# A four-layer graph network on one core: loads reordered, TensorE transposes chosen by site, and the last ten sample pairs scheduled side by side

## The chip, the cores and the metric

The kernel runs on one core of a Trainium2 chip. A core has TensorE (PE, matmuls and transposes, results in PSUM), VectorE (DVE), ScalarE (ACT), GpSimd (POOL) and the queue of SyncE (SP), which here issues every DMA transfer. Each engine runs its own instructions strictly in the order in which they were written out, and waits on semaphores for the others. The metric is the device time of one execution in microseconds (us), the median of several runs.

## The reference

The input x is 64 samples of 256 nodes with 128 features, in fp32, and adj is one 256x256 weighted adjacency matrix. Four layers follow one another, each `x = layernorm(x + f(x, adj))`:

```python
# layer 0: gated graph network, 5 steps
m = adj @ h                                    # used as both m_in and m_out
z = sigmoid([m, m] @ w3.T + b3 + h @ u3.T + bu3)
r = sigmoid([m, m] @ w4.T + b4 + h @ u3.T + bu3)
hv = tanh([m, m] @ w5.T + b5 + (r * h) @ u5.T + bu5)
h = (1 - z) * h + z * hv
# layer 1: semantic graph convolution, A = softmax of edge values over rows
out = (A * I) @ (x @ W[0]) + (A * (1 - I)) @ (x @ W[1]) + bias
# layer 2: attention over the edges of adj, then a graph isomorphism layer
h = x @ Wp + bp
attn = softmax(leaky(s_src + s_dst) where adj > 0)
g = relu(layernorm((attn * adj) @ h))
z = relu(layernorm(((1 + eps) * g + adj @ g) @ W1 + b1))
out = relu(z @ W2 + b2 + g)
# layer 3: polynomials of adj up to the third order
y = sum_k (adj^k @ x) @ V_k                    # k = 0..3
```

## The kernel before

**Tiles.** Two samples make a pair, so there are 32 pairs. A pair's state is a 128x512 fp32 tile: two samples, two halves of the nodes, 128 features. Products with adj need the nodes on the partitions, products with weights need the features there, so a tile is often turned (its four 128x128 blocks transposed).

**A turn** (`turn`, L440 to L479) is made in one of two ways. Through DMA: DVE transposes 32x32 blocks (L467), a transfer writes the tile to a DRAM buffer (L469), four transfers read its blocks back in the turned order (L475). On PE: four transposes against the identity into a PSUM bank (L461), then a copy to SBUF by ACT (L202) or DVE (L203). The sites of turns are named: `h` (the new state after each of layer 0's first four steps), `y` (after the fifth), `x1` (layer 1; on PE it uses `transposes`, L437, and its consumer L629 reads PSUM with no copy), `x2` and `w` (layer 2; `w` is the attention, 1024 columns, two turns), `z` (layer 2's hidden state), `x3` (layer 3). `by_dma` (L449) decides. Before the change all sites of pairs 0 to 29 go through DMA, all sites of pairs 30 and 31 are on PE.

**Stages on PE**, by line:

- L486, `spread`: a product with a 256x256 matrix (adj transposed is `aT`, layer 1's is `offT`, layer 2's is `ginT`).
- L580, L581, L588, L595, L596: layer 0's gate matmuls, 512 columns each; five steps.
- L617, `products`: weights of layer 1 and 2, 128 columns.
- L645: layer 2's first product. L686: attention times features.
- L724, L725, L732: layer 3 (`vx`, `vq`, and `a2T`, the square of adj).

Around them: L584, L590, L598 are the tanh on ACT, L586, L600, L601, L603 the gates' arithmetic on DVE, L500 to L521 and L538 to L567 the layer norms (statistics on DVE or ACT, the power on POOL, the scaling on DVE, ACT or POOL), L654 to L673 the attention's scores, largest value, leaky step and exponential, L691 to L707 the vector work of layer 2, L738 the store of the result.

**Order.** Every operation is added to one list, with its pair, one or more ways (engine and planned duration), the values it reads and writes. `Schedule.order` (L109) then plays the list with those planned durations: again and again it takes, of all operations whose inputs are planned to be ready, the one that can start first, and writes the instructions out in that order. Where two can start together, the smaller `due(pair) - rest` goes first. `rest` is the planned length of what hangs on the operation within its pair. `due` is 20 per pair, but 10 for the last 8 pairs (`DUE`, `LAST_DUE`, `LAST`, L41). An operation that may run on several engines takes the one where it would end first. `MARGIN` stretches planned durations on all engines but PE, and `LAG` is added to what one engine needs to see another's result.

**Buffers.** `CLASSES` (L34) gives the number of tiles: X holds the pairs' states, T their loaded transposes, A the working tiles, B the attention tiles of 1024 columns, E the DRAM buffers of turns, PS the eight PSUM banks. An operation that needs a tile waits in the plan until one is free.

**Start.** `load` (L226) puts the inputs on the SP queue: aT, x of the first pair, W0 (the weights of layer 0), xT of the first pair, the bias columns, pairs 1 and 2, adj, W1 (the other weights), rows. That is the order in which they are added. All have pair -1, whose due is -10000, and the order among them follows `rest`, which puts W0 and the columns ahead. `WARM` dummy matmuls (L255) keep PE active until inputs are there.

Of the kernel before, what the change touches and what calls it, by code (L numbers as in the profile page):

```python
# [14 lines left out]
D = 128  # L15
STEPS = 5

BY_DMA = ("h", "y", "x1", "x2", "w", "z", "x3")
BY_PE = 2

WARM = 6

TURN, TT = 0.44, 0.61
LN_EPS = 1e-5
# [6 lines left out]
N_L0 = 8  # L31
# [1 line left out]
ROWS = ["l1_bias", "bp", "b1", "gat_g", "gat_b", "b2"]  # L33


CLASSES = {"X": (512, 12), "T": (512, 3), "A": (512, 34), "H": (520, 5), "B": (1024, 8), "S": (32, 64), "PS": (512, 8), "D": (512, 4), "E": (1024, 8)}

SEEN = {"PE": 0.23, "ACT": 0.16, "DVE": 0.16, "POOL": 0.12, "SP": 2.5}

USES = {"DVE+": ("DVE", "PORT"), "POOL": ("POOL", "PORT")}  # L40


DUE, LAST_DUE, LAST = 20.0, 10.0, 8

MARGIN, LAG = 1.06, 0.8


def mm(cols):
# [30 lines left out]
class Schedule:  # L79
# [20 lines left out]
        return op  # L100

    def due(self, pair):
        if pair < 0:
            return -1e4
        late = max(pair - (self.n_pairs - LAST), 0)
        return DUE * (pair - late) + LAST_DUE * late

    def order(self, tiles):
        for op in self.ops:  # L109
            op.waits = len(op.before)  # L110
            for b in op.before:
                b.then.append(op)
            for v in dict.fromkeys([*op.reads, *op.writes]):
                v.left += 1
        for op in reversed(self.ops):
            us = min(w[1] for w in op.ways) + op.seen
            op.rest = us + max((x.rest for x in op.then if x.pair == op.pair), default=0.0)
        free = {cls: [(0.0, t) for t in ts] for cls, ts in tiles.items()}
        engines = dict.fromkeys([*SEEN, "PORT"], 0.0)
        ready = [op for op in self.ops if not op.waits]  # L120
        out = []
        while ready:
            best = None
            for op in ready:
                held = 0.0
                for v in op.writes:
                    if v.cls and v.ap is None:
                        held = max(held, min((t for t, _ in free[v.cls]), default=1e9))
                if held == 1e9:
                    continue  # L130
                for engine, us, fn in op.ways:
                    us = us if engine == "PE" else us * MARGIN
                    start = max(op.ready, held, *(engines[e] for e in USES.get(engine, (engine,))))
                    key = (start + (us if len(op.ways) > 1 else 0.0), self.due(op.pair) - op.rest, op.number)
                    if best is None or key < best[0]:
                        best = key, start, op, engine, us, fn
            if best is None:
                raise RuntimeError("no operation can start: too few tiles")
            _, start, op, engine, us, fn = best
            ready.remove(op)  # L140
            for v in op.writes:
                if v.cls and v.ap is None:
                    slot = min(free[v.cls], key=lambda s: s[0])
                    free[v.cls].remove(slot)
                    v.ap = slot[1]
            end = start + us
            engines.update(dict.fromkeys(USES.get(engine, (engine,)), end))
            out.append((start, op.number, op, fn))
            for v in dict.fromkeys([*op.reads, *op.writes]):
                v.left -= 1  # L150
                v.end = max(v.end, end + op.seen)
                if not v.left and v.cls:
                    free[v.cls].append((v.end, v.ap))
            for x in op.then:
                x.waits -= 1
                same = engine != "SP" and x.ways[0][0].rstrip("+") == engine.rstrip("+")
                x.ready = max(x.ready, end + (0.0 if same else op.seen))
                if not x.waits:
                    ready.append(x)

            for v in dict.fromkeys([*op.reads, *op.writes]):
                op.__dict__.setdefault("tiles", {})[v] = v.ap
        assert len(out) == len(self.ops), "operations that wait for one another"
        self.span = max(engines.values())
        return [(op, fn) for _, _, op, fn in sorted(out, key=lambda x: x[:2])]
# [3 lines left out]
def kernel(ctx: ExitStack, tc: tile.TileContext, x, xT, adj, adjT, mats, cols, rows, out):  # L169
    nc = tc.nc  # L170
    n_pairs = x.shape[0] // 2
# [4 lines left out]
    S = Schedule(n_pairs)  # L176

    def fixed(shape, name):
        return Value(ap=const.tile([P, *shape], F32, name=name), name=name)

    def pe(us, fn, r, w):
        S.add([("PE", us, fn)], r, w)
# [4 lines left out]
    def dve(us, fn, r, w):  # L187
        S.add([("DVE", us, fn)], r, w)
# [19 lines left out]
    W0, W1 = fixed([N_L0, D], "W0"), fixed([len(MATS) - N_L0, D], "W1")  # L208
    ccol = fixed([len(COLS)], "ccol")
# [13 lines left out]
        i = ROWS.index(name)  # L223
        return rbc.ap[:, None, i * D:(i + 1) * D].to_broadcast([P, n, D])

    def load(o, i, v):  # L226
        S.add([("SP", 0.4, lambda: nc.sync.dma_start(o(), i))], [], [v])

    xs = [Value("X", name=f"x{p}") for p in range(n_pairs)]
    hTs = [Value("T", name=f"hT{p}") for p in range(n_pairs)]  # L230
# [1 line left out]
    def load_x(p):  # L232
        load(lambda: xs[p].at(4, D), x[2 * p:2 * p + 2].rearrange("b (t p) d -> p (b t) d", p=P), xs[p])
        load(lambda: hTs[p].at(2, N), xT[2 * p:2 * p + 2].rearrange("b d n -> d b n"), hTs[p])
# [3 lines left out]
    dve(0.2, lambda: nc.vector.tensor_scalar(ident.ap, diff.ap, 0.0, None, op0=ALU.is_equal), [diff], [ident])  # L238
    dve(0.1, lambda: nc.vector.memset(neg_half.ap, -0.5), [], [neg_half])
    load(lambda: aT.ap, adjT.rearrange("(t p) i -> p t i", p=P), aT)  # L240
    load(lambda: xs[0].at(4, D), x[0:2].rearrange("b (t p) d -> p (b t) d", p=P), xs[0])
    load(lambda: W0.ap, mats[:, :N_L0], W0)
    load(lambda: hTs[0].at(2, N), xT[0:2].rearrange("b d n -> d b n"), hTs[0])
    load(lambda: ccol.ap, cols, ccol)
    for p in range(1, 3):
        load_x(p)
    load(lambda: a.ap, adj.rearrange("(t p) j -> p t j", p=P), a)
    load(lambda: W1.ap, mats[:, N_L0:], W1)
    load(lambda: rbc.ap, bass.AP(tensor=rows.tensor, offset=rows.offset, ap=[[0, P], [1, n_rows]]), rbc)


# [1 line left out]
    dve(0.3, lambda: nc.vector.memset(ones.ap, 1.0), [], [ones])  # L253
    for _ in range(WARM):
        pe(0.87, lambda: nc.tensor.matmul(idle.at(N), ones.ap[:, :P], ones.ap, start=True, stop=True), [ones], [idle])  # L255
# [191 lines left out]
        return v  # L447

    def by_dma(site):  # L449
        return site in BY_DMA and S.pair < n_pairs - BY_PE  # L450

    def turn(i, name, site, n=512):


        o = Value("A", name=name) if n == 512 else i
        if not by_dma(site):
            ts = [Value("PS", name="ps") for _ in range(n // 512)]
            for k, t in enumerate(ts):
                def fn(k=k, t=t):
                    for c in range(4):  # L460
                        nc.tensor.transpose(tokens(t)[:, c, :], i.at(n // P, P)[:, 4 * k + c, :], ident.ap)  # L461
                pe(TURN, fn, [i, ident], [t])
            for k, t in enumerate(ts):
                evacuate(lambda k=k: o.at(n)[:, 512 * k:512 * k + 512], lambda t=t: t.at(512), [t], [o])
            return o
        st, d = Value("A" if n == 512 else "B", name="turn"), Value("E", name="turn")
        dve(n / 512 * 0.55 + 0.09, lambda: nc.vector.transpose(st.at(n), i.at(n)), [i], [st])  # L467
        blocks = lambda *ap: bass.AP(tensor=d.ap.tensor, offset=d.ap.offset, ap=ap)
        S.add([("SP", 0.4, lambda: nc.sync.dma_start(blocks([P, P], [P * P, n // P], [1, P]), st.at(n // P, P)))],  # L469
              [st], [d], n / 512 * 0.7 + 1.3)  # L470

        def move():
            for q in range(4):
                b = blocks([P, 32], [32 * P, n // 32], [1, 32])
                nc.sync.dma_start(o.at(n // 32, 32)[32 * q:32 * q + 32],  # L475
                                  bass.AP(tensor=b.tensor, offset=b.offset + 32 * q, ap=b.ap))
        S.add([("SP", 2.1, move)], [d], [o], n / 512 * 1.5 + 1.9)
        return o
# [271 lines left out]
    tiles = {}  # L750
    for cls, (n, count) in CLASSES.items():
        where = {"PS": psum, "D": dram, "E": dram}.get(cls, shared)
# [47 lines left out]
```

## Time and profile before

| | |
|---|---|
| time, median of 3 (lowest to highest) | 1554.17 us (1551.33 to 1554.42) |
| span of the profiled run | 1547.6 us |
| PE, DVE, ACT, POOL busy | 1525.6, 1201.5, 868.7, 372.2 us |
| mean granted PE clock | 0.997 |
| DMA traffic | 210.47 MB, 136 GB/s on average |
| HBM read, written | 113.97 MB, 94.96 MB |

An engine's busy time divided by the span is its share. PE's records overlap, since matmuls are pipelined, so its busy time is an upper bound of its work. The page's slices give the busy share of each fortieth of the span in tenths. The chain of waits is followed back from the last instruction and tells which engine's work, at each moment, had to be over for the end to come when it did. A wait names the engine that stood, the line and tile of the instruction that waited, and the one that released it. The windows give each engine's busy time in stretches of the span. Traffic is mostly the turns: each writes 256 KB to DRAM and reads it back.

### The profile page before, as it was taken

The page shows a single profiled execution, that of the slowest core. Times are in us where ns is not written, and L with a number is a line of the kernel's source. Part 1 is how long each engine was busy: PE and PEld are TensorE (multiplying, and loading weights), DVE is VectorE, ACT ScalarE, POOL GpSimd, SP SyncE. Part 2 cuts the span into 40 slices and gives each one's busy share as a digit, 9 for nine tenths or more (in the row PEclk, how much of TensorE's full clock was granted, in tenths as well). Part 3 has the DMA queues.
Part 4 walks back from the last instruction along what each step waited for, and adds up shares of the span by engine and source line. Part 5 has one row for each costly group of instructions (what it writes and reads, how often), then busy time and mean ns, then how long its engine had stood idle before and what let it go on. Part 6 is the DMA issues. An engine that isn't in the chain of part 4 may idle for free.

```text
span 1547.6 us, 22483 instructions
## 1 busy us (share of the span) xinstructions
PE 1525.6 (99%) x6356; PEld 1060.9 (69%) x6356; DVE 1201.5 (78%) x2879; ACT 868.7 (56%) x2363; POOL 372.2 (24%) x467
## 2 busy tenths in 40 slices
PE   9999999999999999999999999999999999999987
PEld 6556666666776666677766677766667767777886
DVE  5556768888888868777788777878787878899874
ACT  3444445566655565565655665565555555667752
POOL 0000110022333121221222222221322312445632
PEclk9999999999999999999999999999999999999999
DMA  7434557777678767677777677877666854557541
GB/s 216 106 72 97 107 113 150 158 146 147 145 165 164 166 134 149 139 145 144 165 145 149 148 132 150 158 144 155 150 137 138 165 114 102 125 107 144 108 92 48
DMA packets 917788, 210.47 MB, mean 136 GB/s; under 512 B 702752, under 2 KB 913184, under 8 KB 917664
## 3 DMA queue, kind: packets, MB, share of 16 engines
q1 hardware_dynamic: 917664, 209.04, 65.3%
q8 instruction: 51, 0.84, 0.2%
q14 instruction: 73, 0.60, 0.1%
HBM read 113.97 MB, written 94.96 MB: 135 GB/s over the span
## 4 chain that ended last, share of the span: by engine, by line
PE 93%; DVE 3%; DMA 2%; SPq 1%; POOL 1%; issue 1%; ACT 0%; POOLq 0%; DVEq 0%; ACTq 0%
PE ps L486 27%; PE ps L596 9%; PE ps L595 9%; PE ps L588 9%; PE ps L580 9%; PE ps L581 9%; PE ps L617 7%; PE ps L724 3%; PE ps L725 3%; PE ps L686 3%; PE ps L732 3%; PE ps L645 2%; DMA W<-mats_in 0%; DMA a<-d 0%; DMA a<-e 0%
## 5 line engine op out<-in xcount | busy, mean ns | idle before, releaser
L202 ACT COPY a<-ps 128x512 f32<-128x512 f32 (+1 forms) x286 | 156.6, 550 | 221.3 <-PE ps L486 167.9
L486 PE MATMUL ps<-aT,a 128*128 128x256 f32 x1024 | 243.9, 379 | 2.6 <-DMA a<-e 1.5
L486 PEld LDWEIGHTS ps<-aT,a 128*128 128x128 f32 x1024 | 192.4, 190 | 64.0 <-issue 38.5
L598 ACT ACTIVATE a<-ps,bzrh 128x512 f32<-128x512 f32 x160 | 109.9, 687 | 173.5 <-PE ps L596 167.9
L584 ACT ACTIVATE a<-ps,bzrh 128x512 f32<-128x512 f32 x160 | 109.7, 686 | 152.0 <-PE ps L581 145.4
L549 POOL TENSOR_SCALAR s<-s 128x4 f32<-128x4 f32 x96 | 30.9, 322 | 607.7 <-ACT a L544 452.8
L596 PE MATMUL ps<-a,u5h 128*128 128x512 f32 x320 | 163.5, 592 | 0.3 <-DVE a L586 0.3
L595 PE MATMUL ps<-a,w 128*128 128x512 f32 x320 | 163.5, 592 | 0.0
L581 PE MATMUL ps<-a,w 128*128 128x512 f32 x320 | 163.4, 592 | 0.0
L588 PE MATMUL ps<-a,w 128*128 128x512 f32 x320 | 163.2, 592 | 0.0
L590 ACT ACTIVATE a<-ps,bzrh 128x512 f32<-128x512 f32 x160 | 109.8, 686 | 88.2 <-PE ps L588 85.3
L617 PEld LDWEIGHTS ps<-W,a 128*128 128x128 f32 x1024 | 129.7, 193 | 28.4 <-issue 25.6
L600 DVE TENSOR_TENSOR a<-a,a 128x512 f32<-128x512 f32 x128 | 89.0, 695 | 72.0 <-ACT a L598 68.9
L552 POOL TENSOR_TENSOR s<-s,neg_half 128x4 f32<-128x4 f32 x128 | 140.3, 1096 | 10.5
L601 DVE SCALAR_TENSOR_TENSOR a<-a,a 128x512 f32<-128x512 f32 x160 | 113.0, 707 | 32.3 <-ACT a L590 28.7
L467 DVE STREAM_TRANSPOSE a<-a 128x512 f32<-128x512 f32 x180 | 126.8, 707 | 5.5 <-ACT a L563 0.3
L617 PE MATMUL ps<-W,a 128*128 128x128 f32 x1024 | 130.9, 276 | 0.0
L580 PE MATMUL ps<-a,W 128*128 128x512 f32 x256 | 130.8, 592 | 0.0
L486 PE MATMUL ps<-aT,x 128*128 128x256 f32 x512 | 123.8, 380 | 1.4 <-DVE x L516 0.8
L486 PEld LDWEIGHTS ps<-aT,x 128*128 128x128 f32 x512 | 95.0, 190 | 28.8 <-issue 17.3
L596 PEld LDWEIGHTS ps<-a,u5h 128*128 128x128 f32 x320 | 60.7, 190 | 77.2 <-issue 65.0
L581 PEld LDWEIGHTS ps<-a,w 128*128 128x128 f32 x320 | 60.8, 190 | 76.5 <-issue 70.8
(183 smaller groups left out, 2709.4 us busy)
## 6 DMA issues: line engine op xcount, KB each, us to landing
e<-a SPq DMA_DIRECT2D x270, 256.0 KB
a<-e SPq DMA_DIRECT2D x1080, 64.0 KB
e<-b SPq DMA_DIRECT2D x30, 512.0 KB
b<-e SPq DMA_DIRECT2D x120, 128.0 KB
x<-x_in SPq DMA_DIRECT2D x32, 256.0 KB
t<-xT_in SPq DMA_DIRECT2D x32, 256.0 KB
a<-d SPq DMA_DIRECT2D x32, 256.0 KB
y_out<-a SPq DMA_DIRECT2D x32, 256.0 KB
```

The source lines that it names most:

```text
L202: S.add([("ACT", us[0], lambda: nc.scalar.copy(o(), i())), ("DVE", us[1], lambda: nc.vector.tensor_copy(o(), i()))], r, w)
L467: dve(n / 512 * 0.55 + 0.09, lambda: nc.vector.transpose(st.at(n), i.at(n)), [i], [st])
L486: nc.tensor.matmul(t.at(2, N)[:, b, :], tokens(i)[:, 2 * b + j, :], right.ap[:, j, :], start=(j == 0), stop=(j == 1))
L552: pool(1.02, lambda: nc.gpsimd.tensor_tensor(rs(), rs(), neg_half.ap, op=ALU.pow), [s, neg_half], [s])
L580: nc.tensor.matmul(t.at(512), mat("u3"), hT.at(512), start=True, stop=False)
L581: nc.tensor.matmul(t.at(512), w345.ap[:, 1, :], mT.at(512), start=False, stop=True)
L588: pe(mm(512), lambda t=t, mT=mT: nc.tensor.matmul(t.at(512), w345.ap[:, 0, :], mT.at(512), start=False, stop=True, skip_group_check=True), ...
L595: nc.tensor.matmul(t.at(512), w345.ap[:, 2, :], mT.at(512), start=True, stop=False)
L596: nc.tensor.matmul(t.at(512), u5h.ap, r.at(512), start=False, stop=True)
L598: act(0.59, lambda t=t, hv=hv: nc.scalar.activation(hv.at(512), t.at(512), AF.Tanh, bias=bzrh.ap[:, 2:3]), [t, bzrh], [hv])
L601: dve2(TT, lambda hv=hv, z=z: nc.vector.scalar_tensor_tensor(hv.at(512), z.at(512), 1.0, hv.at(512), op0=ALU.add, op1=ALU.mult), [hv, z], ...
L617: nc.tensor.matmul(tokens(t)[:, c, :], tokens(i)[:, c, :], w(), start=(k == 0), stop=(k == len(lefts) - 1))
```

## The change

- **Loads.** Operations of pair -1 all get the same rank, so that they go in the order in which they are added: aT and x of the first pair, then W0. Their planned landing times now depend on their size.
- **Warm-up.** Four dummy matmuls in place of six.
- **Turns.** Each site has its own number of last pairs that are turned on PE: `h` 1, `y`, `x1`, `x2`, `x3` 3, `w` 2, `z` 4.
- **Last pairs.** The last ten pairs are due 5 apart, in place of eight 10 apart, so that the end has more pairs in work at once.
- **Tiles.** One more X tile (13), two fewer B tiles (6).
- **Margin.** Planned durations off PE are stretched by 1.03 in place of 1.06.

The purpose is a PE that starts sooner, and that has enough independent work of several pairs at the end.

```diff
-BY_DMA = ("h", "y", "x1", "x2", "w", "z", "x3")
-BY_PE = 2
-
-WARM = 6
+BY_DMA = {"h": 1, "y": 3, "x1": 3, "x2": 3, "w": 2, "z": 4, "x3": 3}
+
+WARM = 4
...
-CLASSES = {"X": (512, 12), "T": (512, 3), "A": (512, 34), "H": (520, 5), "B": (1024, 8), "S": (32, 64), "PS": (512, 8), "D": (512, 4), "E": (1024, 8)}
+CLASSES = {"X": (512, 13), "T": (512, 3), "A": (512, 34), "H": (520, 5), "B": (1024, 6), "S": (32, 64), "PS": (512, 8), "D": (512, 4), "E": (1024, 8)}
...
-DUE, LAST_DUE, LAST = 20.0, 10.0, 8
-
-MARGIN, LAG = 1.06, 0.8
+DUE, LAST_DUE, LAST = 20.0, 5.0, 10
+
+MARGIN, LAG = 1.03, 0.8
...
     def due(self, pair):
-        if pair < 0:
-            return -1e4
         late = max(pair - (self.n_pairs - LAST), 0)
...
-                    key = (start + (us if len(op.ways) > 1 else 0.0), self.due(op.pair) - op.rest, op.number)
+                    late = self.due(op.pair) - op.rest if op.pair >= 0 else -1e4
+                    key = (start + (us if len(op.ways) > 1 else 0.0), late, op.number)
...
-    def load(o, i, v):
-        S.add([("SP", 0.4, lambda: nc.sync.dma_start(o(), i))], [], [v])
+    def load(o, i, v, kb=256):
+        S.add([("SP", 0.45, lambda: nc.sync.dma_start(o(), i))], [], [v], 1.7 + kb / 256)
...
     def by_dma(site):
-        return site in BY_DMA and S.pair < n_pairs - BY_PE
+        return S.pair < n_pairs - BY_DMA[site]
```

In the changed kernel all lines after L99 stand two to three lines earlier, so that L486 becomes L484, and so on.

More of the change, by code (lines that the diff above doesn't have):

```diff
@@ L241 @@
     load(lambda: xs[0].at(4, D), x[0:2].rearrange("b (t p) d -> p (b t) d", p=P), xs[0])
-    load(lambda: W0.ap, mats[:, :N_L0], W0)
+    load(lambda: W0.ap, mats[:, :N_L0], W0, 512)
     load(lambda: hTs[0].at(2, N), xT[0:2].rearrange("b d n -> d b n"), hTs[0])
-    load(lambda: ccol.ap, cols, ccol)
+    load(lambda: ccol.ap, cols, ccol, 16)
     for p in range(1, 3):
@@ L247 @@
     load(lambda: a.ap, adj.rearrange("(t p) j -> p t j", p=P), a)
-    load(lambda: W1.ap, mats[:, N_L0:], W1)
+    load(lambda: W1.ap, mats[:, N_L0:], W1, 832)
     load(lambda: rbc.ap, bass.AP(tensor=rows.tensor, offset=rows.offset, ap=[[0, P], [1, n_rows]]), rbc)
```

## The prediction

> **What bounds the kernel now.** I read the page's first two parts, then the windows by stretch, then the waits and the chain of the last stretch. All times are microseconds.
>
> The page's first part, and the TensorE row of its slices:
>
> ```profile
> PE 1525.6 (99%) x6356; PEld 1060.9 (69%) x6356; DVE 1201.5 (78%) x2879; ACT 868.7 (56%) x2363; POOL 372.2 (24%) x467
> PE   9999999999999999999999999999999999999987
> ```
>
> TensorE (PE) is busy 99%, and its chain share is 93%:
>
> ```profile
> PE 93%; DVE 3%; DMA 2%; SPq 1%; POOL 1%; issue 1%; ACT 0%; POOLq 0%; DVEq 0%; ACTq 0%
> ```
>
> Busy matmuls overlap in the record, so I counted starts instead. Back to back, the two passes of an fp32 matmul start 0.429 apart at 512 columns, 0.216 at 256 and 0.111 at 128. All matmuls at these intervals sum to 1514.5 (1511.9 without the 12 warm-up passes). The first useful one starts at 7.20, the last ends at 1541.3, so 1534.1 - 1511.9 = 22 is lost between them, with 7.2 ahead and 6.3 behind. Adding up each start's excess over its interval says where: 0.7 before 20, 1.7 at 495, 2.1 at 1367 to 1396, and 17.1 after 1426. Everything else is dense. So the change can gain only in those places. The windows show the same (length, then busy PE, PEld, DVE, ACT, POOL, then clock, DMA):
>
> ```profile
> 900.00:1300.00 400.00, 400.00 (x1666) 278.01 (x1665) 313.60 (x745) 226.51 (x624) 96.45 (x122) 1.00 0.69 141
> 1380.00:1426.00 46.00, 44.70 (x246) 36.16 (x245) 42.47 (x134) 33.13 (x113) 25.61 (x31) 1.00 0.65 129
> 1426.00:1480.00 54.00, 45.99 (x268) 40.91 (x268) 46.20 (x129) 37.69 (x138) 29.65 (x35) 0.94 0.59 121
> 1480.00:1541.30 61.30, 58.51 (x303) 50.30 (x301) 37.02 (x130) 24.54 (x79) 19.22 (x28) 1.00 0.26 61
> ```
>
> VectorE (DVE) rises from 78% of the steady stretch to 92% and 86% near the end: layer 0, which is mostly TensorE work, has run out (its last matmul, L596, starts at 1406.3). The waits of the last 120 name what PE stood for:
>
> ```profile
> PE ps L686 <- DVE b L203: 3.9, 1, 3.9
> PE ps L486 <- DVE a L694: 2.0, 1, 2.0
> PE ps L724 <- ACT a L202: 1.4, 2, 0.7
> PE ps L645 <- DVE a L203: 1.3, 1, 1.3
> ```
>
> Two kinds. The first two and the last are work in DVE's in-order queue behind other pairs' work; the chain shows the largest, the PSUM copy L203 behind the score line L660, a product sum L699 and a transpose L467:
>
> ```profile
> 1469.95 0.86 DVE b L660
> ...
> 1471.86 0.60 DVE a L699
> 1472.46 0.62 DVE a L467
> 1473.54 0.78 DVE s L500 x4
> 1474.60 0.58 DVE b L203
> 1475.22 3.48 PE ps L686 x16
> ```
>
> The third kind is order alone: at the very end L724 stands directly behind its own transposes L461 and waits for the copy between.
>
> **What the Trainium skill says.** "TensorE: Matmul & The Clock Gate", Part 1, says an idle window of about 3.4 halves the clock and a busy one restores it. The trace agrees on the size: after the waits that ended at 1429.1 and 1475.2 the record has 3.41 at half clock each (the window's 0.94), costing 1.5 and 1.6 of the 17.1. It differs on what is needed: gaps of 2.0 and 3.9 sufficed, while one of 1.6 at 495 did not. So a shorter tail wait is worth more than itself. "Perfetto Trace Analysis", Optimization Strategy, says that regimes with different busiest engines may gain from interleaving; the windows above show two such regimes.
>
> **The change, part by part.**
>
> *Loads first.* aT and x0 now precede W0 and ccol on the queue. Their spread (L486) can start earlier than 7.20. But the queue is one stream, and the bytes ahead of x1 (W0, ccol, aT, x0, the first xT) are the same set; x1 landed at 8.73 before, when PE needed it at 8.93. The fourth x tile paced PE again:
>
> ```profile
> 7.20 4.55 PE L486 MATMUL ps<-aT,x 128*128 128x256 f32 x20 [0.54 <-DMA x<-x_in]
> 15.94 0.73 PEld L486 LDWEIGHTS ps<-aT,x 128*128 128x128 f32 x4 [0.29 <-DMA x<-x_in]
> ```
>
> It still has the same bytes ahead. So I take -0.3: -1.2 if the cold start of the transfers hides better, +0.8 if W0, landing later than 4.28, holds L581. *Warm-up 6 to 4* (12 passes at 0.427 to 8) ends at 1.17 + 3.4 = 4.6 rather than 6.5. If the clock is still half at x0's spread, this costs 1.7, between x0's landing and x1's: nothing.
>
> *Sites of PE transposes.* Before, 11 turns in each of 2 pairs: 22. After: h 1x4, y 3, x1 3, x2 3, w 2x2, z 4, x3 3: 24. Two more of 4 x 0.109: +0.9 on PE. Each turn moved off DMA takes a 0.7 transpose L467 from DVE and gives a 0.55 copy to ACT or 0.6 to DVE, except x1, whose product reads PSUM directly. It also replaces two transfers (4.39 and 3.39 where the chain crosses them) by about 1.2; the h turns of pair 30 go the other way, with layer 0 of pair 31 beside them.
>
> *Ten pairs spaced 5 instead of eight spaced 10, thirteen x tiles, six B tiles, margin 1.03.* This moves no work on PE but its order. From the instruction lists of the two kernels, with the intervals above: PE has 117 of work left after the last layer-0 matmul before the change, 127 after. I placed every DVE operation by the PE work remaining where the planner's list puts it, priced it from its row, and scaled to the page's 1201.5. Between 120 and 45 from the end, DVE has 82 beside 75 of PE before, and 71 beside 74 after: an excess of 7 becomes room of 3. ACT has 68 and 65. For each tail matmul I took the PE work between it and the PE instruction its operand comes from, minus the chain between them at row durations. Operands with under 1.0 to spare in the last 150: 34 before, 9 after. In the last 25 eight are negative before, one after, because L732 and half a spread now stand between L461 and L724.
>
> Price of the tail. From 1500 on, 4.4 is lost; only the last a2T product keeps its short wait: 0.5, so -3.9. From 1426 to 1480, 12.8 is lost, 3.1 of it clock. The excess of 7 goes, but work is lumpier than sums and ACT is full between 105 and 60 from the end (46 beside 45), so I leave 4.5: -8.3. Bounds: 1.5 left, or 11 left with a clock drop. The stalls at 495 and 1367 to 1396 (3.8) depend on details of the order; my count finds equally few tight operands before the tail in both, so I leave 2.8: -1.0; range -3.5 to +3. The 6.3 behind the last matmul is the same chain of statistics, power, scaling and store: 0. *X and B tiles*: no load or B operation lies on the chain; 0, hidden by PE.
>
> Sum: -0.3 + 0.9 - 3.9 - 8.3 - 1.0 = -12.6, so 1554.2 - 12.6 = **1541.6**.
>
> **Rivals.**
> A, *the waits only move*. ACT takes DVE's place: 28 more L202 copies and nearly full use between 105 and 60. For it: strict queues, and a sum 1 over PE's. Against: ACT was as full before, and no tail wait above 2 was for it. The tail then keeps 11 of 12.8: 1541.6 + 6.5 = 1548.
> B, *slower*: ten pairs in hand and a margin of 3% let the real operations fall behind the plan through the whole run, and PE waits as at 495, eight more times at 1.7 with two clock drops of 1.7: 17. 1541.6 + 17 = 1558.6. For it: the plan spends its spare on ordering. Against: DVE's 78% and ACT's 56% in the dense 1406.
> C, *nothing*: new waits of 12 or 13 in all, ahead of the tail where its work was moved to, take the gain back: 1554. Against: the DVE excess there would have to show in the sums, and does not.
>
> **Chances.** Forecast 0.74 (1536 to 1546), A 0.14, B 0.08, C 0.04. Faster by over 0.2% 0.88, within 0.04, slower 0.08. The forecast's own terms span -19 to -1, its ends unlikely together; with A the range is 1535.5 to 1551, leaving out B, C and small ends.
>
> **What would show it.** Right: after about 1406 the windows have PE at 95% or more, clock 1.00 to the end, no PE wait over 2 for L203 or L694, and no wait of L722 (the old L724) for L200. First spread near 5, but the fourth x tile reached near 15.9. Wrong: half-clock records in the tail, PE waits for ACT there, or a loss of more than 5 between 20 and 1350.

## The result, and the profile after

The changed kernel takes **1531.94 us** (median of 4 runs, 1531.48 to 1532.05) against 1554.14 (1551.33 to 1554.42) before: a ratio of 0.9861, 95% interval 0.9843 to 0.9878. The gain is 22.2 us. The forecast was 12.6, and the time lies below the range. Direction, place and most signs in the trace came as forecast; the size did not.

The page of the changed kernel: TensorE's row of the first part, its row of the slices, and the shares of the chain by engine.

```profile
PE 1518.9 (99%) x6360; PEld 1058.7 (69%) x6360; DVE 1169.8 (76%) x2880; ACT 901.5 (59%) x2403; POOL 354.6 (23%) x446
...
PE   8999999999999999999999999999999999999998
...
PE 98%; DMA 1%; DVE 0%; SPq 0%; POOLq 0%; issue 0%; DVEq 0%; POOL 0%
```

The last two slices were 8 and 7 and are now 9 and 8; the first one was 9 and is now 8. So the end became denser and the start less dense. The chain now runs through PE for 98% of the span, 93% before.

The windows of the changed kernel (stretch, length, busy PE, PEld, DVE, ACT, POOL, then clock and DMA):

```profile
495.00:500.00 5.00, 5.00 (x29) 4.06 (x28) 4.39 (x13) 2.55 (x11) 1.70 (x2) 1.00 0.22 58
...
900.00:1300.00 400.00, 400.00 (x1694) 279.52 (x1693) 317.40 (x785) 238.52 (x652) 100.33 (x123) 1.00 0.72 146
1410.00:1460.00 50.00, 49.91 (x311) 45.40 (x310) 46.22 (x133) 44.70 (x159) 31.76 (x39) 1.00 0.62 130
1460.00:1524.00 64.00, 63.81 (x343) 56.52 (x341) 34.11 (x132) 30.33 (x97) 23.23 (x34) 1.00 0.24 56
```

The third line is the one to look at. DVE is busy 46.22 of 50 (92%), as full as at 1380 to 1426 before the change, ACT 44.70 (89%, there 72%), and PE's records leave 0.09 of 50 uncovered. The clock stays at 1.00.

All waits of PE in the whole span (line waited for, total, times, longest):

```profile
PE ps L484 <- DMA x<-x_in: 3.4, 2, 2.7
PE ps L253 <- DVE ones L251: 1.2, 1, 1.2
PE ps L594 <- DVE a L584: 0.2, 1, 0.2
```

No wait is left but those of the start. The end, in the timeline of before and then of the changed kernel (start, length, engine, line, tiles, in brackets the idle time ahead):

```profile
1534.14 0.60 PE L461 MATMUL ps<-ident,x 128*128 128x128 f32 x4
1535.47 0.70 PE L724 MATMUL ps<-vx,a 128*128 128x256 f32 x2 [0.73 <-ACT a L202]
```

```profile
1508.69 0.60 PE L459 MATMUL ps<-ident,x 128*128 128x128 f32 x4
1509.13 1.89 PE L730 MATMUL ps<-a,a2T 128*128 128x256 f32 x8
1510.86 1.03 PE L484 MATMUL ps<-aT,x 128*128 128x256 f32 x4
1511.72 0.59 PE L722 MATMUL ps<-vx,a 128*128 128x256 f32 x2
```

Before, layer 3's product stands right behind its own transposes and PE waits 0.73 for the copy. After, another sample's a2T product and half a spread fill the 2.6 us between, and no bracket is left.

To locate the difference I count as the prediction did: each matmul start's excess over 0.429, 0.216 or 0.111 us.

| us, profiled execution | before | after | forecast of the difference | measured |
|---|---|---|---|---|
| first useful matmul, plus loss before 50 | 8.06 | 9.63 | -0.3 | +1.6 |
| PE's own work | 1511.9 | 1512.8 | +0.9 | +0.9 |
| loss 450 to 1400 | 3.9 | 0.1 | -1.0 | -3.8 |
| loss after 1400 | 17.14 | 1.05 | -12.2 | -16.1 |
| behind the last matmul | 6.60 | 6.37 | 0 | -0.2 |
| span | 1547.6 | 1530.1 | -12.6 | -17.5 |

The rows differ from the span by rounding and by 0.1 that lies between 50 and 450. After 1400 what is left is many small gaps, 0.87 of it between 1410 and 1460. The table accounts for 17.5 of the 22.2: the profiled execution of before took 1549.42, 4.7 below the median.

### The profile page after: what moved, and what is told of

Its sections match the earlier page's. It is cut to its first block, busy times and chain, and to the rows that moved or that the text cites. A ratio compares the mean times of both kernels' runs of the same rounds, so it can differ in the third digit from the quotient of the medians.

```text
span 1530.1 us, 22320 instructions
## 1 busy us (share of the span) xinstructions
PE 1518.9 (99%) x6360; PEld 1058.7 (69%) x6360; DVE 1169.8 (76%) x2880; ACT 901.5 (59%) x2403; POOL 354.6 (23%) x446
## 4 chain that ended last, share of the span: by engine, by line
PE 98%; DMA 1%; DVE 0%; SPq 0%; POOLq 0%; issue 0%; DVEq 0%; POOL 0%
PE ps L484 29%; PE ps L594 9%; PE ps L593 9%; PE ps L586 9%; PE ps L578 9%; PE ps L579 9%; PE ps L615 7%; PE ps L684 4%; PE ps L722 4%; PE ps L730 4%; PE ps L723 4%; PE ps L643 2%; PE ps L459 1%; DMA rbc<-rows_in 1%; DMA t<-xT_in 0%; PE ps L416 0%
## 5 line engine op out<-in xcount | busy, mean ns | idle before, releaser
L200 ACT COPY a<-ps 128x512 f32<-128x512 f32 (+1 forms) x312 | 169.7, 546 | 183.9 <-PE ps L484 136.5
L484 PE MATMUL ps<-aT,a 128*128 128x256 f32 x1024 | 241.4, 379 | 0.0
L484 PEld LDWEIGHTS ps<-aT,a 128*128 128x128 f32 x1024 | 193.7, 190 | 63.0 <-issue 39.0
L547 POOL TENSOR_SCALAR s<-s 128x4 f32<-128x4 f32 x96 | 42.9, 447 | 622.8 <-DVE s L538 326.3
L594 PE MATMUL ps<-a,u5h 128*128 128x512 f32 x320 | 163.5, 592 | 0.2 <-DVE a L584 0.2
L578 PE MATMUL ps<-a,W 128*128 128x512 f32 x256 | 130.8, 592 | 0.0
L484 PE MATMUL ps<-aT,x 128*128 128x256 f32 x512 | 124.9, 380 | 3.4 <-DMA x<-x_in 3.4
L484 PEld LDWEIGHTS ps<-aT,x 128*128 128x128 f32 x512 | 95.5, 191 | 33.7 <-issue 19.1
L594 PEld LDWEIGHTS ps<-a,u5h 128*128 128x128 f32 x320 | 60.7, 190 | 77.1 <-issue 59.5
```

The source lines that it names most:

```text
L200: S.add([("ACT", us[0], lambda: nc.scalar.copy(o(), i())), ("DVE", us[1], lambda: nc.vector.tensor_copy(o(), i()))], r, w)
L484: nc.tensor.matmul(t.at(2, N)[:, b, :], tokens(i)[:, 2 * b + j, :], right.ap[:, j, :], start=(j == 0), stop=(j == 1))
L578: nc.tensor.matmul(t.at(512), mat("u3"), hT.at(512), start=True, stop=False)
L594: nc.tensor.matmul(t.at(512), u5h.ap, r.at(512), start=False, stop=True)
```

## Experiments

### The kernel before, once more

Edit: none.

> The unchanged kernel. The change gave 22.2 us by the medians, but its profile is only 17.5 us shorter than the profile of before (1547.6 to 1530.1), whose execution took 1549.42 where the others of the same kernel took 1551.3 to 1554.4. Theory A: the missing 4.7 us are in the tail of before, whose waits let the PE clock drop to half for one window of 3.4 us more or fewer; then another profile of the same kernel has the same dense middle (loss under 5 us between 20 and 1400) and a tail loss that differs from 17.1 by several us, with 2 to 4 half-clock records. Theory B: they are in the start or in the middle, where DMA turns land at different times; then the loss between 20 and 1400 differs from 3.8 by several us and the tail stays at 17.

Measured: 1553.23 (1551.09 to 1556.59, 20 runs) beside 1553.28 for 39 more runs of it, 1549.69 to 1557.15; ratio 1.0006 (0.9998 to 1.0014). The executions of one kernel are spread over 7 us, while the changed kernel's four lie within 0.6. The profile here is of an execution at 1556.59, near the long end; that of before, at 1549.42, was just below the shortest of the 39. PE's longest waits in it:

```profile
PE ps L686 <- DVE b L203: 3.9, 1, 3.9
PE ps L486 <- DMA a<-e: 3.0, 1, 3.0
...
PE ps L486 <- DMA x<-x_in: 1.9, 1, 1.9
```

The stretch around 500 in its windows, and then in those of the profiled execution of before:

```profile
495.00:500.00 5.00, 2.21 (x10) 1.41 (x8) 4.53 (x12) 4.06 (x16) 0.77 (x2) 1.00 1.50 143
500.00:510.00 10.00, 9.80 (x24) 5.72 (x25) 3.51 (x6) 2.72 (x5) 2.00 (x2) 0.83 0.47 89
```

```profile
495.00:500.00 5.00, 3.58 (x13) 2.42 (x14) 2.72 (x9) 3.10 (x12) 2.58 (x3) 1.00 0.62 120
```

The wait for a turn's read-back grew from 1.5 to 3.0, and with it came 3.41 us at half clock (the 0.83), which the shorter one had not brought. Between the two executions the start differs by 1.8, the stall near 500 by 3.7 (1.76 and 5.47) and the end by 2.2 (17.14 and 19.30): with 0.4 less between 1340 and 1400 that is the 7.2 between the spans, so neither theory holds alone. "TensorE: Matmul & The Clock Gate", Part 1, of the Trainium skill calls the window free-running, so that the same program meets it at a different place in each execution. These two fit that, and so does the spread: of the 59 executions, the 19 with a mean clock of 0.997 or more have a median of 1551.1, the 10 with 0.994 or less one of 1555.6. The changed kernel, which has no wait after the start, has no half-clock record after it either.

### One part at a time

Each of these is the kernel before with one edit.

The loads and the warm-up alone:

```diff
-WARM = 6
+WARM = 4
-        if pair < 0:
-            return -1e4
...
+                    late = self.due(op.pair) - op.rest if op.pair >= 0 else -1e4
```

> Only the load order, the planned landing times and the four warm-up matmuls of the change. Theory A (the new order starts PE sooner but makes it wait for the second and fourth x tile): the first layer-0 matmul L580 starts at 12.4 rather than 11.6, so the start costs 0.8 us, and the rest of the time is that of before within what a reshuffled order does to the tail (+-4 us): 1551 to 1559. Theory B (the start is worth something): 1550 or less with L580 before 11.6.

The spacing of the last pairs alone:

```diff
-DUE, LAST_DUE, LAST = 20.0, 10.0, 8
+DUE, LAST_DUE, LAST = 20.0, 5.0, 10
```

> Only the last ten pairs due 5 us apart in place of eight 10 apart. Theory A (the tail's DVE excess is spread out by this): the tail loss after the last layer-0 matmul falls from 17 to about 6, time 1541 to 1546. Theory B (the sites of PE transposes do it, by taking DMA round trips and DVE transposes out of the tail): the tail loss stays over 12, time 1550 or more.

The sites alone:

```diff
-BY_DMA = ("h", "y", "x1", "x2", "w", "z", "x3")
-BY_PE = 2
+BY_DMA = {"h": 1, "y": 3, "x1": 3, "x2": 3, "w": 2, "z": 4, "x3": 3}
```

> Only the new sites of PE transposes. Theory A: PE gets 0.9 us more work, the tail loses about 12 in place of 17, time 1549 to 1553. Theory B (the sites do it): the tail loss falls to 6 or less, time 1541 to 1545.

The margin alone:

```diff
-MARGIN, LAG = 1.06, 0.8
+MARGIN, LAG = 1.03, 0.8
```

> Only MARGIN 1.03 in place of 1.06. Theory A (the wait near 495 is a queue of turns that the order of before makes, and the margin alters that order): the loss between 450 and 700 falls from about 4.8 to under 1, the tail stays between 12 and 20, time 1545 to 1550. Theory B (the 495 wait hangs on something else, such as the B tiles): loss there stays at 4 to 5, time 1551 to 1555.

Measured, with the losses of the profiled execution:

| part alone | time (range) | ratio (95%) | start | 450 to 700 | after 1400 |
|---|---|---|---|---|---|
| before | 1553.28 | 1 | 8.1, 9.8 | 1.8, 5.5 | 17.1, 19.3 |
| loads, warm-up | 1544.76 (1541.14 to 1545.07) | 0.9946 (0.9928 to 0.9965) | 8.2 | 4.5 | 10.6 |
| spacing | 1542.46 (1539.32 to 1544.37) | 0.9935 (0.9915 to 0.9955) | 9.6 | 4.6 | 9.5 |
| sites | 1550.12 (1545.68 to 1552.60) | 0.9975 (0.9966 to 0.9984) | 8.6 | 4.8 | 16.5 |
| margin | 1544.49 (1543.21 to 1544.77) | 0.9936 (0.9921 to 0.9952) | 9.7 | 0.0 | 14.1 |

The first row is the surprise. Loads and warm-up act in the first 20 us and leave the start as it was (8.2), yet the kernel is 0.5% faster: its loss *1400 us later* is 10.6 in place of 17.1. The way from the one to the other leads through the planner: other planned landing times move a first choice, and later choices follow from those before them. Played again, the planner gives a list that differs from that of before from its second entry on. Where only the queue is reordered and the list is kept (in the section on the start), the loss after 1400 stays at 1.6 beside the changed kernel's 1.05. The four gains (8.4, 10.1, 3.9 and 9.9 from the ratios, 32 in all) exceed the 22 of the whole, so they are not shares of it.

Which wait is left differs in each. PE's longest beyond 20, in the waits of spacing alone and then of the margin alone:

```profile
PE ps L486 <- ACT x L521: 3.6, 1, 3.6
PE ps L486 <- DMA a<-e: 2.6, 1, 2.6
```

```profile
PE ps L486 <- ACT x L521: 2.9, 1, 2.9
```

ACT's layer-norm scaling is now the longest, where it was DVE's copy L203. The stall near 500 is there in before and in the next three rows, and gone with the margin. It does not hang on the margin alone, though: it stays away when the margin is put back in the changed kernel (next section).

Spacing and sites together:

```diff
-BY_DMA = ("h", "y", "x1", "x2", "w", "z", "x3")
+BY_DMA = {"h": 1, "y": 3, "x1": 3, "x2": 3, "w": 2, "z": 4, "x3": 3}
-DUE, LAST_DUE, LAST = 20.0, 10.0, 8
+DUE, LAST_DUE, LAST = 20.0, 5.0, 10
```

> The kernel before with the new sites and the new spacing of the last pairs together, nothing else. Alone they left tail losses of 16.5 and 9.5. Theory A (they work together: the one gives the tail independent work, the other takes the long chains out of it): tail loss 1 to 5, loss near 495 still 4 to 5.5, time 1536 to 1540. Theory B (they do not add, the rest came from margin and loads): tail loss 7 or more, 1542 or more.

Measured: 1542.83 (1541.89 to 1543.86), ratio 0.9932 (0.9907 to 0.9957): what spacing gives by itself. Loss near 500 4.4, after 1400 8.1. The two parts that the prediction leant on for the end do not bring the end to 1.

### The change less one part

Each of these is the changed kernel with one part put back.

Loads and warm-up as before:

```diff
-WARM = 4
+WARM = 6
+        if pair < 0:
+            return -1e4
...
-                    late = self.due(op.pair) - op.rest if op.pair >= 0 else -1e4
```

> The whole change without its loads: old load order and planned landing, six warm-up matmuls. Theory A (loads are worth nothing): start cost (time of the first useful matmul plus what is lost before 50) 8 to 10 as in the changed kernel's 9.6, tail loss under 4, time 1530 to 1535. Theory B (the order that the new planned landings bring about carries part of the gain, as the 8 us of loads alone suggest): tail loss or the loss near 495 comes back with 4 or more, time 1536 or more.

Eight pairs spaced 10:

```diff
-DUE, LAST_DUE, LAST = 20.0, 5.0, 10
+DUE, LAST_DUE, LAST = 20.0, 10.0, 8
```

> The whole change with the last eight pairs due 10 apart again. Theory A (the spacing is the larger part of the tail's gain): tail loss 7 to 12, time 1538 to 1544. Theory B (sites and the rest suffice): tail loss under 4, 1531 to 1535.

All turns of pairs 30 and 31 on PE, and no others:

```diff
-BY_DMA = {"h": 1, "y": 3, "x1": 3, "x2": 3, "w": 2, "z": 4, "x3": 3}
+BY_DMA = ("h", "y", "x1", "x2", "w", "z", "x3")
+BY_PE = 2
```

> The whole change with the old sites: all turns of the last two pairs on PE and none other. PE has 0.9 us less work. Theory A (the sites are the smaller part): tail loss 3 to 6, time 1533 to 1537. Theory B (DMA turns of x1, x2, z and x3 in pairs 28 and 29 are what makes PE wait at the end): tail loss over 8, 1539 or more.

The margin as before:

```diff
-MARGIN, LAG = 1.03, 0.8
+MARGIN, LAG = 1.06, 0.8
```

> The whole change with MARGIN 1.06 again. Theory A (the margin alone removed the wait near 495 and had little to do with the tail): the loss between 450 and 700 is back at 4 to 5.5, tail loss under 4, time 1536 to 1540. Theory B (what took the tail to 1 us is one lucky order among many, and any change of a planned duration draws another): tail loss 5 to 12 as well, 1541 or more.

A third of the way there:

```diff
-MARGIN, LAG = 1.03, 0.8
+MARGIN, LAG = 1.04, 0.8
```

> The whole change with MARGIN 1.04, a small disturbance of the plan. Theory A (the tail's gain comes from spacing and sites): tail loss under 4, no loss over 1 near 495, time 1531 to 1535. Theory B (order luck): tail loss 5 or more, 1536 or more.

The tiles as before:

```diff
-CLASSES = {"X": (512, 13), "T": (512, 3), "A": (512, 34), "H": (520, 5), "B": (1024, 6), "S": (32, 64), "PS": (512, 8), "D": (512, 4), "E": (1024, 8)}
+CLASSES = {"X": (512, 12), "T": (512, 3), "A": (512, 34), "H": (520, 5), "B": (1024, 8), "S": (32, 64), "PS": (512, 8), "D": (512, 4), "E": (1024, 8)}
```

> The whole change with 12 X and 8 B tiles again. Theory A (no tile lies on the path): 1531 to 1535, tail loss under 4. Theory B (ten pairs side by side need the thirteenth X tile): a wait of pair 31's start or of the tail of 3 or more, time 1535 to 1540.

Measured, beside VectorE's work as in the prediction (from the instruction lists, placed between 120 and 45 us of PE's work before the end, in which PE itself has 74 to 76):

| put back | time (range) | ratio (95%) | loss after 1400 | DVE in the stretch |
|---|---|---|---|---|
| nothing: the change | 1531.94 (1531.48 to 1532.05) | 0.9861 (0.9843 to 0.9878) | 1.05 | 71 |
| loads, warm-up | 1537.34 (1537.10 to 1538.27) | 0.9893 (0.9878 to 0.9908) | 6.1 | 78 |
| spacing | 1540.26 (1539.64 to 1540.88) | 0.9911 (0.9896 to 0.9926) | 9.1 | 82 |
| tiles | 1541.56 (1541.34 to 1542.82) | 0.9926 (0.9901 to 0.9950) | 10.7 | 80 |
| margin 1.04 | 1544.22 (1541.44 to 1545.51) | 0.9942 (0.9922 to 0.9961) | 10.8 | 78 |
| margin 1.06 | 1544.26 (1543.18 to 1545.91) | 0.9944 (0.9926 to 0.9962) | 10.5 | 78 |
| sites | 1550.83 (1549.49 to 1552.54) | 0.9986 (0.9978 to 0.9993) | 16.4 | 82 |

Every part seems to be needed, even a margin of 1.03 rather than 1.04, which exists only in the plan. Each time the end falls back to a loss of 6 to 16, and mostly for another reason. The column leaves out two of the waits below, the one for L644 (at 1346) and the one for L484 with margin 1.06 (at 1399.6); and the profile of margin 1.04 is of its shortest execution, 1541.44. The old tiles fit neither theory: slower than both allowed. PE's longest waits beyond the start, in order: old sites (its lines stand one later), margin 1.06, margin 1.04, old tiles.

```profile
PE ps L616 <- ACT a L701: 6.5, 3, 4.0
PE ps L644 <- DMA a<-e: 3.4, 1, 3.4
```

```profile
PE ps L722 <- DMA a<-e: 6.8, 1, 6.8
...
PE ps L484 <- ACT x L519: 3.0, 1, 3.0
```

```profile
PE ps L615 <- POOL s L503: 3.6, 1, 3.6
```

```profile
PE ps L730 <- DVE a L201: 2.7, 3, 1.3
...
PE ps L684 <- DMA b<-e: 1.8, 1, 1.8
```

ACT, a turn through DRAM, POOL, DVE: no one engine is behind all of them. And PE can starve beside engines with time to spare. The windows of margin 1.04:

```profile
1410.00:1460.00 50.00, 43.62 (x264) 38.66 (x263) 37.61 (x123) 39.23 (x128) 27.67 (x34) 1.00 0.60 111
```

DVE has 37.61 of 50 and ACT 39.23, both well below the 46.22 and 44.70 of the changed kernel, and PE loses 6.4. Busy shares don't tell the good order from the bad one.

Two readings remain after this table: the last column does separate the whole change (71) from all others (78 to 82), so room on DVE could still be the cause. ACT's sum does not separate them: by planned durations it has 64 in that stretch in the changed kernel and 57 to 73 in the others. The next pair tests DVE's.

### More work for VectorE in the same order

Both are the changed kernel with its list of instructions kept and additions put between VectorE's own in the stretch of the last column:

```diff
-        for op, fn in S.order(tiles):
+        extra = {5636, 5686, 5728, 5786, 5817, 5851, 5897, 5938, 5983}
+        for k, (op, fn) in enumerate(S.order(tiles)):
...
+            if k in extra:
+                nc.vector.tensor_tensor(kf.ap, ones.ap, ones.ap, op=ALU.add)
```

> The changed kernel with its order kept, and 9 VectorE additions more (128x256 of ones into a tile that nobody reads), spread evenly among VectorE's own instructions where the order list has 120 down to 45 us of PE's work to go. VectorE has 71 us of listed work there beside PE's 74; each addition takes about 0.37 us by the groups of like size, so some 3.3 us are added. Theory A, VectorE's capacity in that stretch sets what PE loses at the end (kernels with 78 to 82 us there lose 6 to 19 us, the changed one with 71 loses 1): the loss after 1400 becomes 1.5 to 4, the time 1532.5 to 1535. Theory B, the order of the hand-overs sets it and VectorE's sum has slack enough: the loss stays under 2, the time 1531.5 to 1533.

The same with 18 positions:

> As the one before with 18 such additions, some 6.7 us, which brings VectorE's listed work in the stretch to 78 us beside PE's 74, where the neighbours of the changed kernel stand that lose 6 to 11 us at the end. Theory A: the loss after 1400 becomes 5 to 9, the time 1536 to 1540. Theory B: under 4, the time at most 1535; the neighbours' losses then come from their order and not from VectorE's sum.

Measured: with 9 additions 1532.46 (1530.87 to 1532.69), ratio 0.9861 (0.9842 to 0.9880), with 18 of them 1532.45 (1531.96 to 1532.89), ratio 0.9864 (0.9849 to 0.9879). The median addition took 0.41 (0.414 with 18), so by the median they are 3.7 and 7.5 us, more than expected, and bring the 71 to 75 and 78 (two of the 18 took 0.89 and 1.49, which makes their sum 9.0). The windows and PE's waits after 1380, with 18:

```profile
1410.00:1460.00 50.00, 48.68 (x301) 44.09 (x300) 48.67 (x141) 42.42 (x151) 30.29 (x36) 1.00 0.57 122
```

```profile
PE ps L615 <- ACT a L700: 1.0, 1, 1.0
PE ps L484 <- ACT a L691: 0.3, 1, 0.3
```

VectorE is busy 97% there, and the loss after 1400 grows from 1.05 to 1.51 and 2.45, not to 5 to 9. So VectorE's sum, brought to where three neighbours stand that lose 6 to 11 (loads and both margins), explains 1.4 us of that; the rest lies in their lists, which place the same kind of work differently. The reading by capacity falls as far as this goes: a sum of 82 was not put into the good order, but the two kernels with 82 lose 9.1 and 16.4, so the sum doesn't set the loss there either.

### The start

Only the queue of loads as before (the changed kernel's order of everything else is kept):

```diff
+        load_order = ['W0', 'ccol', 'aT', 'x0', 'hT0', 'x1', 'hT1', 'x2', 'hT2', 'a', 'W1', 'rbc']
...
+        for k, entry in zip(sorted(load_at.values()), load_moved):
+            plan[k] = entry
```

> The changed kernel with its order kept and only the load queue in the order of before (W0 and the columns first). Theory A (the change's load order is worth nothing or costs a little, as its start cost of 9.6 against 8.1 to 9.8 says): 1530.5 to 1532.2, L578 between 11.5 and 12.5. Theory B (it gains what it was made for): 1533 or more.

Measured: 1531.91 (1531.18 to 1532.44), ratio 0.9861 (0.9848 to 0.9875); changed kernel 1531.94. **The new order of loads by itself is worth nothing.** L578 began at 13.58, later than theory A had it, since this profile has 3.41 us of half clock at 8.1; the first L594 still came at 20.45, beside 20.74. The beginning in the timeline, of the changed kernel and then of this one:

```profile
4.78 2.30 PE L484 MATMUL ps<-aT,x 128*128 128x256 f32 x8
...
9.74 2.86 PE L484 MATMUL ps<-aT,x 128*128 128x256 f32 x12 [2.67 <-DMA x<-x_in]
12.44 1.02 PE L578 MATMUL ps<-t,W 128*128 128x512 f32 x2
...
16.49 0.55 DVE L272 TENSOR_REDUCE s<-rbc 128x3 f32<-128x384 f32 x1 [1.98 <-DMA rbc<-rows_in]
...
17.66 1.13 PE L484 MATMUL ps<-aT,x 128*128 128x256 f32 x4 [0.76 <-DMA x<-x_in]
...
20.00 0.68 DVE L584 SCALAR_TENSOR_TENSOR a<-a,t 128x512 f32<-128x512 f32 x1
...
20.74 1.12 PE L594 MATMUL ps<-a,u5h 128*128 128x512 f32 x2 [0.23 <-DVE a L584]
```

```profile
7.50 6.24 PE L484 MATMUL ps<-aT,x 128*128 128x256 f32 x20 [2.58 <-DMA x<-x_in]
13.58 1.02 PE L578 MATMUL ps<-t,W 128*128 128x512 f32 x2
```

PE does start 2.7 earlier, and then stands 2.67 for x of the second pair, behind W0 in the queue. In the ten profiles with this order of loads that wait is between 1.1 and 3.1. A second limit shows in the DVE lines: VectorE's queue holds setup work on the late `rows`, stands 1.98 for it, and the gate L584, which frees the first L594, has to come after it.

Three versions take up these two. x of three pairs ahead of W0 in the queue:

```diff
+        load_order = ['aT', 'x0', 'x1', 'x2', 'W0', 'hT0', 'ccol', 'hT1', 'x3', 'hT2', 'a', 'W1', 'rbc']
```

> The changed kernel with its order kept, the first three x tiles ahead of W0 and the fourth ahead of adj, VectorE's setup left in its place. Theory A (without moving the setup, VectorE waits for the rows, which land 0.9 us later, before the gate L584, so the x tiles gain little): L578 near 10.5 but L594 not before 21, time 1531 to 1532.5. Theory B (the queue alone is the pace): 1529.5 or less.

The setup work that waits for W1 and `rows` behind the second L584 on VectorE:

```diff
+        plan_late = [k for k in range(plan_gate) if plan[k][0].pair <= 0 and plan[k][0].ways[0][0].startswith("DVE")
+                and {v.name for v in plan[k][0].writes} & {"W1", "rbc", "mean", "wpx", "vx", "vq", "hbias"}]
```

> The changed kernel with its order kept, but VectorE's setup that needs W1 or the rows moved behind the first two L584. Theory A (the queue paces PE first): the wait of L594 for L584 goes, worth 0.4, and no more: 1531.4 to 1531.8. Theory B (the in-order setup is the pace): 1530 or less.

Both:

> The changed kernel with its planned order kept, but the first three x tiles ahead of W0, the fourth ahead of adj, and VectorE's setup that needs W1 or the rows moved behind the first two L584. Theory A (the queue paces PE until about 16 and VectorE's setup, waiting for the rows until 16.5, after that): L578 starts near 10.5 rather than 12.4, the gate L584 near 17, start cost 6 to 7 rather than 9.6, time 1528.5 to 1529.5. Theory B (bytes are bytes: the later W0 takes back what the earlier x gives): start cost 9 to 10, time 1531.5 to 1532.5.

Measured, all in one comparison: x first 1532.41 (1531.62 to 1534.24), ratio 0.9867 (0.9853 to 0.9880); setup later 1531.33 (1530.92 to 1532.11), 0.9859 (0.9845 to 0.9872); both **1528.55** (1527.54 to 1528.87), 0.9839 (0.9826 to 0.9853). Timeline with x first, and with both:

```profile
19.94 2.08 PE L594 MATMUL ps<-a,u5h 128*128 128x512 f32 x2 [3.08 <-DVE a L584]
```

```profile
9.79 1.10 PE L578 MATMUL ps<-t,W 128*128 128x512 f32 x2 [0.42 <-DMA t<-xT_in]
...
16.94 1.02 PE L594 MATMUL ps<-a,u5h 128*128 128x512 f32 x2
```

With x first, layer 0 begins at 9.53 rather than 12.44, and all of it is given back in 3.08 at L594 and the half clock behind it (6.8 us in that profile, which is of the longest of the four executions). With setup later alone, PE still waits for x. Removing either limit uncovers the other; removing both brings the first L594 from 20.74 to 16.94 and the time down by 3.4. This is the fastest version here.

## Why the prediction was wrong

- **What bounds the kernel**: right. The trace had named the places, and the loss went in those places and in no other.
- **Loads, -0.3**: right in the time, as the experiment on the queue alone shows (0.0), though the fourth x tile came at 17.66 and not near 15.9. "x1 landed at 8.73 before, when PE needed it at 8.93" did not carry over: it landed at 9.70 after, though the bytes ahead of it are the same. W0's packets started between 3.44 and 7.44 after the change, and between 1.76 and 3.75 before. The +1.6 in the table is no effect of the change in the median: the start of before is 8.06 in one profiled execution and 9.81 in the other.
- **Two more turns, +0.9**: right (1511.9 to 1512.8).
- **The stalls at 495 and 1367 to 1396, -1.0**: mis-sized; 3.8 of 3.9 went. "My count finds equally few tight operands" looked at PE's distance to its producers in the list, but the wait near 500 is for a turn's read-back through DRAM, and how full the DMA engines are is not in such a list (the windows have a DMA share, a sum of packet times that can pass 1, of 0.62 and 1.50 with the wait, 0.22 without). It also varied from 1.8 to 5.5 between executions of one kernel.
- **From 1500 on, -3.9**: right. L724's wait for its copy went for the reason given.
- **From 1426 to 1480, "so I leave 4.5: -8.3"**: the step of the argument that failed. 1.05 is left in the whole end. Two inputs were wrong. I took VectorE's excess of 7 as the cause; 7.5 us put back into the same order costs 1.4. And I left 4.5 for lumpiness as if sums set it; lists with the same sum of 78 lose from 2.45 to 10.8, so what PE loses there is set by the list, and the changed one has almost no bad place. That it came out so well was not foreseen: with a margin of 1.04 instead of 1.03 the loss is 10.8. The lower bound that I gave, 1.5, was near it.
- **The base**: failed too, and is the largest single difference. 1554.2 is a median, but the losses subtracted from it were those of one execution of 1549.42. It missed 4.7 of losses that the median execution has and that the change removes too (3.9 by the median of 1553.28 over 59 executions). A hint was there beforehand: the span of 1547.6 is 3.7 below the *lowest* timed run, 1551.33. In the changed kernel the profiled execution's span and time, 1530.1 and 1531.83, differ by 1.8.

Together: +1.9 (start), -2.8 (stalls), -3.9 (end), -0.2 and -4.7 (base) make -9.7, the whole difference between 1541.6 and 1531.9.

Of the rivals, A (waits move to ACT) did not come in the changed kernel, but it is what several of its neighbours do: spacing alone has 3.6 for L521, old sites 6.5 for L701. All signs that were to show the forecast right at the end were there: PE above 95% after 1406, clock at 1.00, no waits for L203, L694 or L200. "Perfetto Trace Analysis", Optimization Strategy, of the skill says that interleaving regimes may gain; the change does that and the loss at the end went, but spacing alone, which does it too, leaves 9.5 of it.

**What stays open.** That the planned list sets the end, and not VectorE's sum (up to the 78 put in), is shown; which property of a list makes it good is not. A list is an order and a choice of engines, and the two were not separated: played again, the planner with margin 1.04 picks another engine for 233 of the 978 operations that may run on either of two. The count of operands with under 1.0 us to spare in the last 150 is lowest but one in the changed kernel (9, and 34 before), but spacing with sites has 5 and loses 8.1. Nor is it shown that the five parts have a merit of their own beyond this draw of the order. The median execution of before was not profiled, so the 4.7 is placed by the two at the ends of its spread.

## What to carry to other kernels

Where a planner writes the order, compare kernels and not edits: an edit that touches a planned time can draw a new order for everything behind the first choice that it moves, so switching one part on or off tells the worth of a draw. How far back that goes differs: with margin 1.04 the list leaves that of the changed kernel at entry 44 of 6157, with the spacing alone it keeps the first 3958 of 6162 of before. To price a part by itself, keep the list fixed and change only that, as the experiments on the load queue and on VectorE's work do. Before subtracting losses from a time, check where the profiled execution lies among the timed ones. And when a faster start gains nothing, look for the second limit right behind the first, and lift both.

## What the runs showed of the hardware

- **Where a gap of PE falls decided whether the clock dropped, not its length alone.** In all 20 profiles the clock records change only on a grid of 3.41 us, with a phase of its own in each. After every one of the 23 full-clock grid windows in which PE stood 1.99 us or more, the next window was at half clock; with 1.5 to 1.98 it was so in 5 of 22 cases, with less in none. So a gap of 3.59 (margin 1.04, at 1458.7) brought no drop, split 1.98 and 1.61 over two windows, and one of 1.52 (loads put back, at 1439.1) did. "TensorE: Matmul & The Clock Gate", Part 1, puts the drop after an idle window of about 3.4; here less was enough.
- **An in-order queue at 97% need not slow its consumers much**: VectorE was busy 48.67 of 50 us with 18 additions more, and PE's records leave 1.3 of that stretch uncovered, 0.09 without the additions.
- **The same bytes in another order of the queue did not take the same time**: W0's 128 packets of 4 KB started within 2.0 to 2.2 us when they came first (eight profiles). Behind aT and x they took 3.1 to 4.0 in nine profiles and 2.2 in the tenth (loads alone). In the changed kernel it was 4.0, with one packet taking 2.27 us where the usual one took 0.159.
